# Causal attention whose exponentials are shifted by one maximum for four heads and 512 queries, with a checked general path

## The chip, the cores and the metric

The kernel runs on one core of one Trainium2 chip. The metric is the device time of one launch in microseconds. Five engines of the core work in parallel, each through its own instructions in program order: TensorE (PE in the profile, with its weight loads shown apart as PEld), VectorE (DVE), ScalarE (ACT), GpSimd (POOL) and SyncE (SP), which here issues almost all transfers. Three launches of the kernel before took 2398.28, 2401.68 and 2404.61 us.

## The reference, cut to what matters

The input has 4096 tokens of 256 features. An attention with 16 heads of 16 features and a feed-forward network follow each other, each between two layer norms and with a residual:

```python
qkv = x @ w_attn + b_attn
q, k, v = jnp.split(qkv, 3, axis=-1)              # then 16 heads of 16 features
logits = jnp.einsum('bhqd,bhkd->bhqk', q, k) * scale
logits = jnp.where(causal[None, None, :, :], logits, -jnp.inf)
weights = jax.nn.softmax(logits, axis=-1)
out = jnp.einsum('bhqk,bhkd->bhqd', weights, v)
return out.reshape(b, n, d) @ w_proj + b_proj
...
x = x + _layernorm(attention(_layernorm(x)))
x = x + _layernorm(feed_forward(_layernorm(x)))   # 256 -> 1024 -> 1024 -> 1024 -> 256
```

A softmax row doesn't change when one number is subtracted from all its logits before the exponentials. The number that is usually taken is the row's own maximum; any other number serves as long as the exponentials neither overflow nor all vanish. The logits of the reference's inputs, worked out from these inputs with the reference's own arithmetic, lie between about -0.75 and 0.75.

## The kernel before, in words

**Tiling.** The 4096 tokens are cut into 8 blocks `j` of 512 queries (`QB`), the 16 heads into 4 groups `g` of four heads. One *item* is a pair `(j, g)`; there are 32, done in the order of `j`, then `g`. An item runs over its keys in *key steps* `kt` of 128 keys: `4 (j + 1)` of them, since the attention is causal, and 576 in all. The last four key steps of an item lie on the diagonal and have 512, 384, 256 and 128 queries left.

**What one key step computes.** `ScoreUnit` (L711 on) makes the logits of two heads at a time, keys on the partitions and queries along the row; a key step has two such units. Its `products` (L729) issues for each head a product of keys and queries (`s<-q,k`) and accumulates a second product onto it (`s<-mrow,ones`): `mrow` holds minus the row maximum of every query, split in two halves, and the product with a tile of ones subtracts it from the logits. ScalarE then takes the exponential from PSUM to the tile `e` (L744), GpSimd zeroes the upper triangle on the diagonal (L749), and two key steps later `Values.step` (L779) multiplies `e` with the values of the four heads and accumulates into the PSUM tile `av`. A column of ones among the values gives the sum of the exponentials, in row 16 of each head's 32 rows. After an item's last key step `av` is copied (L789) and stored (L791).

**Where the row maxima come from.** Before an item's exponentials can start, the maxima of its rows must be known. `MaxUnit` computes the same logits once more with queries on the partitions (L624, tile `pm`, a ring of three PSUM banks) and reduces them along the keys on VectorE (L658; on the diagonal L662, a custom instruction that adds a mask and takes the maximum). In part of the key steps (`hold`, L643) ScalarE first copies one of the four banks to SBUF, and VectorE reduces the copy (L647); that happens only where no other work was lent to ScalarE since (`lent`). At the end of a query tile four maxima per row are combined (L675); at the end of an item they are split into halves (L681 to L686), and `to_rows` turns them to rows by four small products (L694, tile `pmt`) and a copy on ScalarE (L703, `mrow`).

**The order.** It is written out by hand. While item `n` runs, the maxima of item `n+1` are issued, one pair of `MaxUnit`s (four reductions) per key step, and `LEAD` = 3 pairs of the item after it. Per key step the program has: the first `MaxUnit`, two `ScoreUnit`s, the second `MaxUnit`, and the values of two key steps earlier. `to_rows` comes when the counter `now`, which rises by 2 per key step, has advanced by 4 since the maxima ended. `Background` puts pieces of other work between key steps: layer norm, q, k and v of the block two ahead (`prep`), projection and second layer norm of the last block (`project`), and a rounding of the feed-forward weights on GpSimd that sets a flag (`halve_weights`, `count_low`); some of these pieces run a `MaxUnit` beside them. SP's queue carries, in program order, the key and query loads (L495), the stores of q and k (L488), the stores of `av` (L791) and the transfers of `project`, whose sums go to DRAM and come back broadcast over partitions (L252, L257, L262).

**The end.** `feed_forward` is built twice, behind a branch on the flag: with weights that fit the fast fp32r format (`halves`), or without. The first is the one that runs here.

## Time and profile before

The profiled execution took 2401.19 us; its span is 2399.5 us, so 1.7 us lie around it, and it stands 0.5 us under the median of the three launches (2401.68 us). The table gives busy times in four parts of the span. The cuts are the starts of three copies of `av` (L789): that of the last item of block 1, of the last item but one, and of the last. Each copy starts some two key steps after its item's last one, so the count of key steps is meant to within two.

| part | us | PE busy | DVE busy | ACT busy | key steps |
|---|---|---|---|---|---|
| blocks 0 and 1, with the set-up | 269.68 | 220.33 | 158.94 | 123.72 | 48 |
| blocks 2 to 7, all items but the last | 1400.62 | 1378.63 | 1258.95 | 1170.82 | 496 |
| last item (no maxima left to compute) | 65.94 | 65.73 | 0.00 | 59.49 | 32 |
| feed-forward and end | 663.26 | 653.37 | 350.23 | 160.30 | - |
| profiled span | 2399.50 | | | | 576 |

Busy time is the union of an engine's instructions. Two instructions that follow each other without a wait overlap a little (the next starts before the results of the last are written), so the time from start to start is shorter than the duration that a row gives. Matmul ends are modelled.

### The profile page before, as it was taken

To read this page: it belongs to the slowest core of one execution; us is meant where nothing else is said; L and a number is where in the kernel's file an instruction comes from. 1 tells how busy PE (TensorE), PEld (TensorE's weight loads), DVE (VectorE), ACT (ScalarE), POOL (GpSimd) and SP (SyncE) were. 2 spreads that over 40 slices of the span, in tenths; PEclk is the share of its full clock that TensorE was granted. 3 is DMA by queue.
4 is the path that set the end of the run, shared out by engine and by line. 5 is a ranking of instruction groups with operands and counts; after the bars stand their busy time and mean duration, and the time that the engine had idled before them with its cause. 6 is when DMAs were issued, how large, how long until landed. Compare 5 with 4: busy or idle time off the path is not lost.

```text
span 2399.5 us, 40893 instructions
## 1 busy us (share of the span) xinstructions
PE 2318.1 (97%) x15237; PEld 1408.6 (59%) x15237; DVE 1768.1 (74%) x4102; ACT 1514.3 (63%) x2087; POOL 565.9 (24%) x898
## 2 busy tenths in 40 slices
PE   4889999999999999999999999999999999999998
PEld 2545554455554555545555555544488888888887
DVE  1667887998999899988999998986056546544653
ACT  1447787887797888888899888976822222222221
POOL 2324334432334223243223321010002100000000
PEclk8879999999999999999999999999999999999999
DMA  4443534433332432244323232111021000000000
GB/s 144 159 151 123 176 101 159 138 115 106 112 97 96 145 123 75 97 159 120 111 77 96 81 115 62 54 54 62 7 97 46 27 1 18 18 18 1 18 9 11
DMA packets 134831, 202.78 MB, mean 85 GB/s; under 512 B 14912, under 2 KB 59584, under 8 KB 134624
## 3 DMA queue, kind: packets, MB, share of 16 engines
q1 hardware_dynamic: 132672, 198.75, 25.4%
q8 instruction: 122, 2.00, 0.4%
q10 hardware_dynamic: 1776, 1.18, 0.2%
q14 instruction: 85, 0.70, 0.1%
q0 software_dynamic: 176, 0.15, 0.1%
HBM read 137.91 MB, written 62.13 MB: 83 GB/s over the span
## 4 chain that ended last, share of the span: by engine, by line
PE 87%; DVE 6%; ACT 2%; DMA 2%; POOL 1%; issue 1%; SPq 0%; ACTq 0%; POOLq 0%; DVEq 0%
PE av L779 21%; PE s L729 19%; PE z L1090 19%; PE pm L624 15%; PE pyf L1172 2%; PE za L1090 2%; PE zb L1090 2%; DVE mx L658 2%; DVE pm L662 2%; PE py L280 1%; PE pk L465 1%; PE pv L586 1%; PE pq L465 1%; PE pmt L694 1%; ACT e L744 1%
## 5 line engine op out<-in xcount | busy, mean ns | idle before, releaser
L744 ACT ACTIVATE e<-s 128x1024 f32<-128x1024 f32 (+3 forms) x1175 | 1039.7, 936 | 101.0 <-PE s L729 90.5
L658 DVE TENSOR_REDUCE mx<-pm 128x1 f32<-128x512 f32 x1496 | 963.1, 685 | 132.1 <-PE pm L624 90.8
L624 PEld LDWEIGHTS pm<-k,q 64*128 64x128 f32 x2304 | 301.2, 186 | 498.6 <-DVE mx L658 344.4
L624 PE MATMUL pm<-k,q 64*128 64x512 f32 (+3 forms) x2304 | 569.8, 439 | 22.8 <-DVE mx L658 11.7
L779 PE MATMUL av<-e,v 128*32 128x512 f32 (+3 forms) x4608 | 580.3, 575 | 0.6 <-POOL e L749 0.6
L729 PE MATMUL s<-q,k 64*128 64x512 f32 (+3 forms) x2304 | 465.2, 389 | 9.6 <-ACT e L744 2.0
L729 PE MATMUL s<-mrow,ones 64*128 64x512 f32 (+3 forms) x2304 | 452.6, 379 | 0.0
L1157 ACT ACTIVATE fb<-z,sh 128x512 f32<-128x512 f32 x128 | 88.3, 690 | 364.8 <-PE z L1090 339.5
L729 PEld LDWEIGHTS s<-q,k 64*128 64x128 f32 x2304 | 230.6, 187 | 79.8 <-issue 17.8
L662 DVE CUSTOM_DVE_ANT_0 pm<-pm,mask 128x128 f32<-128x128 f32 (+3 forms) x463 | 212.6, 499 | 73.1 <-PE pm L624 68.1
L749 POOL TENSOR_SCALAR_AFFINE_SELECT e<-e 128x256 f32<-128x256 f32 x256 | 103.0, 411 | 682.4 <-ACT e L744 680.7
L729 PEld LDWEIGHTS s<-mrow,ones 64*128 64x128 f32 x2304 | 234.3, 187 | 37.1 <-ACT mrow L703 0.5
L643 ACT COPY held<-pm 128x512 f32<-128x512 f32 (+1 forms) x345 | 200.2, 580 | 50.2 <-PE pm L624 17.7
L647 DVE TENSOR_SCALAR_CACHE_REDUCE held<-held 128x512 f32<-128x512 f32 x296 | 200.1, 676 | 0.1
L1090 PE MATMUL z<-hb_0h,h 128*128 128x512 f32 x512 | 199.3, 389 | 0.0
L1090 PE MATMUL z<-hb_0l,h 128*128 128x512 f32 x512 | 199.2, 389 | 0.0
L779 PEld LDWEIGHTS av<-e,v 128*32 128x32 f32 x4608 | 91.6, 108 | 145.5 <-issue 129.0
L202 POOL TENSOR_TENSOR rstd<-ve,neghalf 128x4 f32<-128x4 f32 (+1 forms) x22 | 20.8, 945 | 632.9 <-DVE ve L200 607.4
L1057 DVE CAST hb_1h<-fb 128x512 fp32r<-128x512 f32 x64 | 27.3, 427 | 156.0 <-ACT fb L1157 156.0
L1134 ACT ACTIVATE sl<-za,s 128x512 f32<-128x512 f32 x64 | 44.0, 690 | 120.0 <-PE za L1090 58.2
L1090 PEld LDWEIGHTS z<-hb_0l,h 128*128 128x128 f32 x512 | 96.1, 188 | 19.9
L1090 PEld LDWEIGHTS z<-hb_0h,h 128*128 128x128 f32 x512 | 96.1, 188 | 19.9
(251 smaller groups left out, 2553.6 us busy)
## 6 DMA issues: line engine op xcount, KB each, us to landing
k<-k SPq DMA_DIRECT2D x288, 256.0 KB
q<-q SPq DMA_DIRECT2D x64, 256.0 KB
x<-in_x_dram SPq DMA_DIRECT2D x16, 512.0 KB
k<-hik SPq DMA_DIRECT2D x32, 256.0 KB
k<-lok SPq DMA_DIRECT2D x32, 256.0 KB
q<-hiq SPq DMA_DIRECT2D x32, 256.0 KB
q<-loq SPq DMA_DIRECT2D x32, 256.0 KB
avd<-av_sb SPq DMA_DIRECT2D x32, 256.0 KB
```

The lines of the kernel that those rows point to most:

```text
L465: nc.tensor.matmul(ps, lhsT=wqk[d][:, i * D + c * P : i * D + (c + 1) * P], rhs=xTs[j][:, d, :], start=(d == 0), stop=(d == DC - 1),)
L624: nc.tensor.matmul(ps[:, 0:n], lhsT=qT[j, g][pr][r, t * P : (t + 1) * P], rhs=kT[G * j + g, c, pr][r, 0:n], start=True, stop=True,)
L643: nc.scalar.copy(held[:, 0:n], ps[:, 0:n])
L647: nc.vector.tensor_scalar(held[:, 0:n], held[:, 0:n], -3.0e38, None, ALU.max, ALU.max, accum_out=self.mx[:, h, c : c + 1],)
L658: nc.vector.tensor_reduce(self.mx[:, h, c : c + 1], ps[:, 0:n], AX.X, ALU.max)
L662: nc.vector.tensor_tensor_reduce(out=ps[:, 0:n], in0=ps[:, 0:n], in1=mask[:, QB - n : QB], scale=1.0, scalar=-3.0e38, op0=ALU.add, op1=ALU ...
L729: nc.tensor.matmul(self.ps[i][:, self.q0 :], lhsT=(self.k, ones[pr])[m][r, :], rhs=(qT[j, g][pr], mT[j, g])[m][r, self.q0 :], start=(m == ...
L744: nc.scalar.activation(e[:, at : at + n, q0:], ps[:, :, q0:], AF.Exp)
L749: nc.gpsimd.affine_select(out=at, in_=at, compare_op=ALU.is_ge, fill=0.0, base=0, pattern=[[0, 2], [1, P]], channel_multiplier=-1,)
L779: nc.tensor.matmul(self.av[h * HW : (h + 1) * HW, q0:], lhsT=vb[kt // NT][:, kt % NT, o : o + HW], rhs=es[h // 2][:, h % 2, q0:], start=(k ...
L1090: nc.tensor.matmul(ps, lhsT=w[c], rhs=single(part[:, c, :]), start=(c == 0 and i == 0), stop=(c == kc - 1 and i == parts - 1),)
L1157: nc.scalar.activation(h, z, AF.Gelu, scale=sc[:, oc : oc + 1])
```

## The change

The second product onto the logits goes, and with it the rows of maxima. An item gets one number for its four heads and 512 queries: the maximum over all the logits that `MaxUnit` computes (the mask on the diagonal goes too, so this includes keys after the query). It is applied as a per-partition bias of the exponential on ScalarE. To find it, VectorE reduces an item's maxima to one per partition (`col`), the 128 numbers go to DRAM and come back broadcast to all partitions (`all`), and VectorE reduces again with the sign turned (`shift`). The program now runs four pairs of maxima ahead instead of three, the last reduction comes 6 counts of `now` after the maxima instead of 4, and in the last two items one pair is issued in every key step until none is left.

Since one shift for many rows can let a row's exponentials vanish, the smallest entry of each row of `av` is kept (`least`), and early in the feed-forward it is tested against 2^-12 where the row is a sum (`tell_distant`). At the end the result is loaded into a register; if any sum was too small, the whole program is run once more by the attention with row maxima (the old code, now `attention(False)`) and the general feed-forward, both built into the same program behind that branch.

The diff without the lines that only moved to the right:

```diff
+        nc.vector.tensor_scalar(sums, sums, 1.0e-30, None, ALU.max)
         nc.vector.reciprocal(sums, sums)
...
+    def tell_distant():
+        nc.vector.tensor_reduce(close, least, AX.X, ALU.min)
+        nc.vector.tensor_scalar(close, close, LEAST, None, ALU.is_ge)
+        nc.vector.tensor_tensor(close, close, other, ALU.max)
+        yield True
+        nc.sync.dma_start(out=lows.rearrange("o p -> p o"), in_=close)
+        row = const.tile([1, P], F32, tag="row", name="row")
+        nc.sync.dma_start(out=row, in_=lows)
+        for _ in range(4):
+            yield True
+        total = stat.tile([1, 1], F32, tag="total", name="total")
+        nc.vector.tensor_reduce(total, row, AX.X, ALU.add)
+        nc.vector.tensor_scalar(distant, total, float(P), None, ALU.is_lt)
+        yield True
...
-    xT0 = []
+    def attention(shared):
+        xT0, W = [], {}
...
-        vb, qT, mT = [], {}, {}
+            ones, identr, mask = (None,) * 3 if shared else constants()
+            vb, qT, mT, shifts = [], {}, {}, {}
+            lead, WAIT = (4, 6) if shared else (LEAD, 4)
...
+                if shared:
+                    mx = top.tile([P, 4 * NT * NB], F32, tag="mx_all", name=f"mx_{j}_{g}")
+                    for t in range(NT):
+                        for c in range(j + 1):
+                            n = QB if c < j else (t + 1) * P
+                            yield [(j, g, t, c, pr, n, mx) for pr in (1, 0)]
+                    return
...
                     heads.append((h, held))
+                    if shared:
+                        return self.overall(heads, held if hold else None)
...
+                def overall(self, heads, held):
+                    j, g, t, c, pr = self.at
+                    mx, n = self.mx, self.n
+                    for h, ps in heads:
+                        at = 4 * (t * (j + 1) + c) + h
+                        if ps is held:
+                            nc.vector.tensor_scalar(
+                                ps[:, 0:n], ps[:, 0:n], -3.0e38, None, ALU.max, ALU.max,
+                                accum_out=mx[:, at : at + 1],
+                            )
+                        else:
+                            nc.vector.tensor_reduce(mx[:, at : at + 1], ps[:, 0:n], AX.X, ALU.max)
+                    if not (pr == 0 and self.diagonal and t == NT - 1):
+                        return False
+                    col = stat.tile([P, 1], F32, tag="col", name=f"col_{j}_{g}")
+                    nc.vector.tensor_reduce(col, mx[:, 0 : 4 * NT * (j + 1)], AX.X, ALU.max)
+                    nc.sync.dma_start(out=highest[j * G + g, :, None], in_=col)
+                    self.all = top.tile([P, P], F32, tag="all", name=f"all_{j}_{g}")
+                    nc.sync.dma_start(out=self.all, in_=highest[j * G + g].partition_broadcast(P))
+                    return True
+
             def to_rows(self):
+                    if shared:
+                        j, g = self.at[:2]
+                        shift = shifts[j, g] = stat.tile([P, 1], F32, tag="shift", name=f"shift_{j}_{g}")
+                        nc.vector.tensor_reduce(shift, self.all, AX.X, ALU.max, negate=True)
+                        return
...
-                for m in range(2):
+                    for m in range(1 if shared else 2):
...
-                            lhsT=(self.k, ones[pr])[m][r, :],
-                            rhs=(qT[j, g][pr], mT[j, g])[m][r, self.q0 :],
+                                lhsT=ones[pr][r, :] if m else self.k[r, :],
+                                rhs=(mT[j, g] if m else qT[j, g][pr])[r, self.q0 :],
                             start=(m == 0),
-                            stop=(m == 1),
+                                stop=(shared or m == 1),
...
-                    nc.scalar.activation(e[:, at : at + n, q0:], ps[:, :, q0:], AF.Exp)
+                        nc.scalar.activation(
+                            e[:, at : at + n, q0:],
+                            ps[:, :, q0:],
+                            AF.Exp,
+                            **({"bias": shifts[j, g]} if shared else {}),
+                        )
...
                     nc.sync.dma_start(out=weighed[j][g], in_=av_sb)
+                        if shared:
+                            at = j * G + g
+                            nc.vector.tensor_reduce(
+                                least[:, at : at + 1], av_sb, AX.X, ALU.min
+                            )
...
-                rows_due.append((now + 4, unit))
+                    rows_due.append((now + WAIT, unit))
...
-        while issued < first[1] + LEAD:
+            while issued < first[1] + lead:
...
-        rows_of(now + 4)
+            rows_of(now + WAIT)
...
                 due = begun + (goal - begun) * (kt + 1) // count[n] - issued
+                    if shared and goal == first[-1]:
+                        due = min(begun + kt + 1, goal) - issued
...
+                if j == 0 and tell:
+                    bg.add("distant", tell_distant(), 8)
...
+    ahead = attention(True)
     low = nc.values_load(flag, min_val=0, max_val=1)
     with tc.If(low < 1) as either:
-        feed_forward(True)
+        feed_forward(True, *ahead, True)
     with either.Else():
-        feed_forward(False)
+        feed_forward(False, *ahead, True)
+    far = nc.values_load(distant, min_val=0, max_val=1)
+    with tc.If(far > 0):
+        feed_forward(False, *attention(False))
```

## The prediction

> **What bounds the kernel now.** I read the page's busy times first, then busy times by stage, then one key step in the timeline.
>
> ```profile
> PE 2318.1 (97%) x15237; PEld 1408.6 (59%) x15237; DVE 1768.1 (74%) x4102; ACT 1514.3 (63%) x2087; POOL 565.9 (24%) x898
> ```
>
> PE looks like the only bound. But the change touches the attention alone, and there the shares are different (columns: us, then busy us and instructions of each engine; granted clock, DMA share, GB/s):
>
> ```profile
> 0.00:269.68 269.68, 220.33 (x1253) 118.88 (x1254) 158.94 (x512) 123.72 (x207) 91.55 (x160) 0.87 0.45 150
> 269.68:1670.30 1400.62, 1378.63 (x10342) 712.95 (x10340) 1258.95 (x2886) 1170.82 (x1576) 418.36 (x670) 1.00 0.32 104
> 1670.30:1736.24 65.94, 65.73 (x504) 25.98 (x500) 0.00 (x0) 59.49 (x85) 3.22 (x8) 0.99 0.02 9
> ```
>
> In the long middle part PE is 98% busy, DVE 90% and ACT 84%. So an edit that takes work from PE alone meets DVE soon. One key step of that part, in the timeline (start, us, engine, line):
>
> ```profile
> 1002.11 0.59 ACT L643 COPY held<-pm 128x512 f32<-128x512 f32 x1
> 1002.64 1.94 ACT L744 ACTIVATE e<-s 128x1024 f32<-128x1024 f32 x2
> 1002.75 0.68 DVE L647 TENSOR_SCALAR_CACHE_REDUCE held<-held 128x512 f32<-128x512 f32 x1
> 1003.17 1.06 PE L779 MATMUL av<-e,v 128*32 128x512 f32 x8
> 1003.35 2.08 DVE L658 TENSOR_REDUCE mx<-pm 128x1 f32<-128x512 f32 x3
> ...
> 1004.17 0.50 PE L624 MATMUL pm<-k,q 64*128 64x512 f32 x2
> 1004.50 0.39 PE L729 MATMUL s<-q,k 64*128 64x512 f32 x2
> 1004.70 0.59 ACT L643 COPY held<-pm 128x512 f32<-128x512 f32 x1
> 1004.74 0.39 PE L729 MATMUL s<-mrow,ones 64*128 64x512 f32 x2
> ```
>
> From one held copy to the next is 2.59 us. In it PE is busy all the time, DVE 2.49 us and ACT 2.47 us (the same busy times by stage, for 1002.11 to 1004.70). I call it a hold step; the middle part has 332 of them (count of L643 in it). All three engines are full there. The other 164 of its 496 key steps take 1400.62 - 332 x 2.59 = 541 us, 3.30 us each: those carry pieces of other work on PE, or are narrow.
>
> **The change, part by part.** All sums are against the profiled 2401.2 us, 0.5 below the median.
>
> *Taken from PE.* From 1004.50 to 1004.74 is 0.23 us for a pair of products, and a full key step has two pairs with `mrow`: 0.46 us. `pmt` (L694) takes 15.7 us of the middle part.
>
> *Added to ACT.* The exponential gets a bias that is read per partition. No exponential has one now. The nearest rows are the layer norm's passes, without and with such a bias, and a copy and an Identity with one:
>
> ```profile
> L643 ACT COPY held<-pm 128x512 f32<-128x512 f32 x322 | 189.1, 587 | 48.7 <-PE pm L624 17.7
> L180 ACT ACTIVATE junk<-y,mvy 128x256 f32<-128x256 f32 x28 | 14.2, 508 | 0.5
> L172 ACT ACTIVATE junk<-y 128x256 f32<-128x256 f32 x28 | 11.6, 416 | 0.7
> L474 ACT ACTIVATE fullk<-pk,bqk 128x512 f32<-128x512 f32 x16 | 11.0, 688 | 36.5 <-PE pk L465 36.5
> ```
>
> 508 - 416 = 92 ns and 688 - 587 = 101 ns. I take 93 ns per exponential; if an exponential's bias were free, the bound is 0. The middle part has 995 exponentials: +92.5 us on ACT, less 13.5 for the `mrow` copies (L703). ACT goes from 1171 to 1250 us.
>
> *DVE keeps its load.* The four reductions per key step stay. Gone are L675 (16.1 us in the middle part) and L681 to L686 (19.3 us in all 32 items, 14 in the 23 items here); added are 23 `least` reductions (as L647, 0.68: 16 us) and 46 small ones (as L675's, some 0.2: 9 us). On the diagonal a plain reduction of 512 (685 ns) stands for the masked one (711); narrower ones I take as 26 ns shorter too: 16 x 23 of them, -10 us. DVE stays near 1244 us. So the middle part, PE-bound at 1379 of 1401, becomes one with ACT 1250, DVE 1244 and PE about 1379 - 212 - 16 = 1151. (Each item has three narrow steps; the pairs there shrink with the queries, by some 0.70 us for the three together. 427 full steps x 0.46 plus 23 x 0.70 is 212.).
>
> *Hold steps (332).* ACT, without a wait, needs 0.53 (1002.11 to 1002.64) plus twice an exponential from start to start: 1.94 less the last one's 1.02 is 0.92, plus 0.093, so 2.56 us, against 2.59 now. Thus at best -0.03 x 332 = -10. If ACT's waits stay as they are, each step grows by 0.19: +62. I take -7, near the lower end, since what ACT waits for is PE, which now has 0.46 us to spare; DVE's 2.49 lies below.
>
> *The other 164 steps.* PE's saving there is 95 full steps x 0.46 + 23 x 0.70 = 60 us. Around an `mrow` copy two key steps took 1012.47 to 1018.38, 5.91 instead of 5.18; without it 0.73 x 23 = 17. Of these 77 us all come off if PE sets each of these steps, none if DVE does. DVE has 1259 - 332 x 2.49 = 432 of 541 us there; after -77 it would be 93% busy, more than work in such pieces reaches elsewhere in the part (90%). I take two thirds, -51; bounds -77 and 0.
>
> *The new wait.* `shift` waits on DVE, in program order, for two transfers through DRAM in sequence. Behind it stand all later reductions, and behind those the `pm` banks and PE; ACT's next item waits for the shift itself. SP holds its later loads meanwhile. No such tiny store exists; `project` sends sums the same way, in the chain of waits and in SP's timeline:
>
> ```profile
> 158.93 2.55 DMA sums<-avd
> 162.08 1.42 DMA invd<-sums
> ```
> ```profile
> 277.83 0.32 SPq L257 DMA_DIRECT2D invd<-sums x1
> 278.19 0.63 SPq L261 DMA_DIRECT2D oo<-avd x1
> 281.71 0.57 SPq L262 DMA_DIRECT2D To<-invd x1
> ```
>
> A store lands after 1.42 us, or as late as 281.71 - 277.83 = 3.88; a load takes 2.55. The round trip is 4.0 to 6.4 us. The count of 6 leaves two full key steps between `col` and `shift`, 5.2 us. The wait is 0 to 1.2 us, 23 times: 0 to 28. I take 0.4, 9 us, as most trips have the short store.
>
> The Trainium skill ("DMA: Bandwidth & Descriptors", Specifications) says that runs under 512 bytes are written by read-modify-write, which speaks against this store of 4-byte pieces. No row here shows its price. The same page (Anatomy of one DMA) gives some 2.0 us fixed per transfer for GpSimd's path; two would be an estimated 4.0 us and no wait.
>
> *The start (0 to 269.68).* Half of L729's 55.83 us there and 7.3 of `pmt` go from a PE that is 82% busy; I take 12 of these 35. The first shifts are needed at once: a round trip of 4.0 to 6.4 us, uncovered, where a product and a copy stood: +5. Together -7; bounds -30 and +8.
>
> *The last item.* ACT has 84 exponentials: 59.49 + 7.8 = 67.3 us, over the present 65.94: +2; bounds -2 and +8.
>
> *The end.* Each engine loads the flag and jumps over the general program; the present load took 0.5 us and PE's jump over the other feed-forward 3.8. Mostly beside the last store: +2; bounds 0 and +8. `tell_distant` runs in the feed-forward, where DVE is 53% busy: 0, or at most its 5 small operations.
>
> Sum: -7 - 51 + 9 - 7 + 2 + 2 = -52: **2349 us**.
>
> **The clock.** PE becomes sparser. The profile grants 0.57 at 132.59 to 156.13, where PE ran 100 products in 23.5 us (4.2 per us), but 1.00 at 213.08 to 248.77 with 214 in 35.7 (6.0 per us). A hold step will have 16 in 2.56 us, 6.2. I take no loss. The skill ("TensorE: Matmul & The Clock Gate", HAM oscillation) warns of PE gaps over about 3.4 us; the waits above are shorter.
>
> **The rivals.**
> - *ScalarE becomes the pole.* The held copy is ACT's own work, so in a hold step the waits for `pm` come after it and don't shrink: +62 instead of -7 gives 2418. For it: 2.56 against 2.59 leaves nothing for jitter. Against: PE's 0.46. It decides from 52/332 = 0.16 us more per hold step than the 2.57 I take, that is from 2.73 us.
> - *The round trip is late.* SP holds the store behind others that wait for GpSimd, or the small pieces are slow. At 10 us (the chain's 6.63 us for a broadcast load, `To`, plus 3.88) the wait is 4.8 x 23 = 110 instead of 9: 2450. It pays back the whole gain from (52 + 9)/23 = 2.7 us of wait, a trip of 7.9. Against: SP's other waits point to older instructions.
> - *PE's saving comes through.* The middle part at DVE's floor, 1259: -142, and the rest -3: 2256. Against: DVE idles now in spite of a full queue.
> - *The general path runs.* Then the time about doubles. The inputs' logits lie within 0.75, so a sum is at least e^-1.5 = 0.22, far above 2^-12. Under 0.005.
>
> **How the numbers follow.** Forecast (2290 to 2390) 0.56; PE's saving through 0.07; terms that cancel to within 0.3% (7 us, about what this measurement can tell) 0.08; ScalarE as pole 0.15; late round trip 0.14. Faster 0.56 + 0.07 = 0.63, same 0.08, slower 0.29. The range leaves out most of the saving-through case and the worse half of the late trips: 2290 to 2430.
>
> **What would show it.** L744's 1024-wide mean near 1115 ns; hold steps at 2.55 to 2.60 us; no `s<-mrow`; PE near 85% in the middle part, DVE and ACT both above 91%; idle time before `shift` on DVE of some 10 us. I am wrong if ACT's mean doesn't move, if hold steps pass 2.7, if DVE's idle before `shift` passes 60 us, or if the granted clock drops after 270 us.

## The result, and the profile after

The changed kernel takes 2749.46 us (median of four launches, 2737.81 to 2759.22) against 2401.93 us for the kernel before on the same chip: a ratio of 1.1446, 95% interval 1.1399 to 1.1493. It is slower by 14%; forecast were 2349 us, and 2290 to 2430 us as the range. The profiled execution has a span of 2756.8 us, 357 more than before; it lies 10 us above the median of the four launches.

Busy times by stage of the changed kernel, cut at the same three copies of `av` as before (columns: us; busy us and instructions of PE, PEld, DVE, ACT, POOL; granted clock, DMA share, GB/s):

```profile
0.00:365.60 365.60, 226.24 (x1024) 107.41 (x1024) 151.60 (x335) 126.27 (x198) 89.10 (x156) 0.74 0.35 113
365.60:2011.10 1645.50, 1443.44 (x8263) 567.78 (x8261) 1233.77 (x2488) 1226.01 (x1566) 413.36 (x669) 0.89 0.27 88
2011.10:2077.90 66.80, 65.73 (x376) 18.23 (x376) 0.69 (x1) 63.87 (x86) 3.22 (x8) 0.96 0.11 39
2077.90:2756.80 678.90, 656.58 (x3144) 552.12 (x3144) 351.92 (x712) 160.03 (x223) 53.01 (x61) 0.99 0.08 24
```

Against before, the start has 96 us more, the middle part 245, the last item 1 and the feed-forward with the end 16. In the middle DVE's and ACT's busy times are near what was forecast (1234 and 1226 us, for 1244 and 1250). But PE runs some 2000 products less and is busy 65 us *longer* (1443 for 1379), at a granted clock of 0.89 where it had 1.00, and it stands for 202 us of the part where it stood for 22. Nothing has become full; everything waits, and PE runs slowly besides.

What is waited for, from the view of waits of the same profile (engine, line, releaser: us in total, times, longest):

```profile
PEld pm L674 <- DVE mx L758: 704.0, 695, 9.2
DVE shift L773 <- DMA all<-highest: 243.3, 30, 20.0
PEld pm L674 <- ACT held L693: 86.8, 312, 1.0
DVE least L883 <- ACT av_sb L878: 92.3, 32, 66.1
PE pm L674 <- DMA k<-k: 72.5, 5, 29.7
```

The first row existed before (344.4 us in 480 waits); it has doubled, in good part because VectorE itself stands in the second (without the trip, in e3_on_chip below, the first row is 485.1 us). The kernel before has no wait like the last row's, of PE for keys. One stand of VectorE, in the timeline (start, us, engine, line, operation; in brackets the idle time before and its releaser):

```profile
1426.96 0.27 DVE L762 TENSOR_REDUCE col<-mx 128x1 f32<-128x112 f32 x1
...
1427.26 0.32 SPq L763 DMA_DIRECT2D highest<-col  x1
...
1431.75 0.50 PE L674 MATMUL pm<-k,q 64*128 64x512 f32 x2
...
1432.17 1.13 PE L292 MATMUL py<-wp,oo 128*128 128x256 f32 x4
...
1433.23 0.49 PE L674 MATMUL pm<-k,q 64*128 64x512 f32 x1
1434.79 0.32 SPq L765 DMA_DIRECT2D all<-highest  x1
1439.57 0.28 DVE L773 TENSOR_REDUCE shift<-all 128x1 f32<-128x128 f32 x1 [7.50 <-DMA all<-highest]
1439.77 2.47 DVE L758 TENSOR_REDUCE mx<-pm 128x1 f32<-128x512 f32 x4
...
1440.51 0.79 PE L674 MATMUL pm<-k,q 64*128 64x512 f32 x1 [6.78 <-DVE mx L758]
...
1441.23 2.07 PE L292 MATMUL py<-wp,oo 128*128 128x256 f32 x4
...
1443.23 0.79 PE L674 MATMUL pm<-k,q 64*128 64x512 f32 x2
```

SP issues the store of 128 numbers at 1427.26, and its next instruction, the load, goes out only when the store has landed: 1434.79, 7.53 us later. From the load's issue to `shift` it is 4.78 us. The whole trip is 12.3 us against 5.2 us of cover. VectorE stands for 7.50 us, and behind it PE for 6.78. After the stand the same products take longer: one pair of `pm` 0.79 instead of 0.50 us, four `py` products 2.07 instead of 1.13. The clock has fallen, and it stays at one half for the next 27 us, in which PE is busy again for 26.3 (the same columns as above):

```profile
1440.50:1467.40 26.90, 26.32 (x99) 11.73 (x99) 15.88 (x29) 12.01 (x20) 6.68 (x10) 0.50 0.46 156
1467.40:1480.00 12.60, 12.60 (x86) 4.78 (x82) 11.44 (x24) 11.91 (x14) 5.45 (x8) 1.00 0.21 69
```

Taken together, the trace's clock record has 582 us at half clock in this launch, in 43 stretches of 3.4 to 47.8 us; before, it has 88 us in 8.

SP's queue stands too, and the key loads behind it. The last row of the waits, at the second shift of block 0:

```profile
120.29 0.32 SPq L763 DMA_DIRECT2D highest<-col  x1
127.81 0.32 SPq L765 DMA_DIRECT2D all<-highest  x1
128.62 0.79 SPq L537 DMA_DIRECT2D q<-q  x2
129.46 1.32 SPq L537 DMA_DIRECT2D k<-k  x2
...
136.39 0.47 PE L674 MATMUL pm<-k,q 64*128 64x128 f32 x2 [17.01 <-DMA k<-k]
```

The loads of the next keys stand in the program behind the store, which has to wait for `col`, and behind the load of the maxima, which waits 7.52 us for the store; PE stands for 17.01 us. In the start PE stands 64.9 us in four such places.

The Trainium skill ("TensorE: Matmul & The Clock Gate", HAM oscillation), which the forecast set aside because its waits were to be short, warns of gaps over about 3.4 us; the trace agrees, with a gap of 6.78 us and products at 0.79 for 0.50 us behind it, and by the clock record 28 of the launch's 30 gaps over 5 us have the clock fall to one half, in the gap or within 3.5 us behind it.

### The profile page after: what moved, and what is told of

It reads as the page before. It is cut to its first block, busy times and chain, and to the rows that moved or that the text cites. A ratio compares the mean times of both kernels' runs of the same rounds, so it can differ in the third digit from the quotient of the medians.

```text
span 2756.8 us, 35602 instructions
## 1 busy us (share of the span) xinstructions
PE 2392.0 (87%) x12805; PEld 1245.6 (45%) x12805; DVE 1738.0 (63%) x3535; ACT 1576.2 (57%) x2069; POOL 558.7 (20%) x894
## 4 chain that ended last, share of the span: by engine, by line
PE 68%; DMA 17%; DVE 8%; ACT 4%; issue 2%; POOL 1%; SPq 0%; ACTq 0%; POOLq 0%; DVEq 0%
PE av L868 17%; PE z L1189 17%; PE pm L674 15%; DMA highest<-col 9%; PE s L813 8%; DMA all<-highest 5%; DVE mx L758 5%; PE pyf L1273 2%; PE za L1189 2%; PE zb L1189 2%; ACT e L828 2%; PE py L292 1%; PE pk L507 1%; PE pv L628 1%; DVE held L748 1%
## 5 line engine op out<-in xcount | busy, mean ns | idle before, releaser
L758 DVE TENSOR_REDUCE mx<-pm 128x1 f32<-128x512 f32 (+3 forms) x1946 | 1151.4, 633 | 317.0 <-PE pm L674 263.2
L828 ACT ACTIVATE e<-s,shift 128x1024 f32<-128x1024 f32 (+4 forms) x1176 | 1142.9, 1038 | 237.0 <-PE s L813 207.6
L674 PE MATMUL pm<-k,q 64*128 64x512 f32 (+3 forms) x2304 | 758.1, 491 | 280.7 <-DVE mx L758 204.7
L674 PEld LDWEIGHTS pm<-k,q 64*128 64x128 f32 x2304 | 354.8, 201 | 927.5 <-DVE mx L758 704.0
L868 PE MATMUL av<-e,v 128*32 128x512 f32 (+3 forms) x4608 | 639.9, 617 | 1.9 <-POOL e L838 1.0
L813 PEld LDWEIGHTS s<-q,k 64*128 64x128 f32 x2304 | 240.2, 203 | 181.5 <-ACT e L828 119.8
L748 DVE TENSOR_SCALAR_CACHE_REDUCE held<-held 128x512 f32<-128x512 f32 (+1 forms) x358 | 239.0, 668 | 0.5
L773 DVE TENSOR_REDUCE shift<-all 128x1 f32<-128x128 f32 x32 | 9.1, 285 | 243.3 <-DMA all<-highest 243.3
L929 POOL CAST wh<-wc 128x256 fp32r<-128x256 f32 x88 | 34.9, 396 | 295.1 <-DMA wc<-in_h_t_dram 203.9
L1156 DVE CAST hb_0h<-fb 128x512 fp32r<-128x512 f32 x64 | 27.5, 430 | 95.5 <-ACT fb L1258 95.5
```

Source lines behind the costliest of these rows:

```text
L674: nc.tensor.matmul(ps[:, 0:n], lhsT=qT[j, g][pr][r, t * P : (t + 1) * P], rhs=kT[G * j + g, c, pr][r, 0:n], start=True, stop=True,)
L748: nc.vector.tensor_scalar(ps[:, 0:n], ps[:, 0:n], -3.0e38, None, ALU.max, ALU.max, accum_out=mx[:, at : at + 1],)
L758: nc.vector.tensor_reduce(mx[:, at : at + 1], ps[:, 0:n], AX.X, ALU.max)
L813: nc.tensor.matmul(self.ps[i][:, self.q0 :], lhsT=ones[pr][r, :] if m else self.k[r, :], rhs=(mT[j, g] if m else qT[j, g][pr])[r, self.q0 ...
L828: nc.scalar.activation(e[:, at : at + n, q0:], ps[:, :, q0:], AF.Exp, **({"bias": shifts[j, g]} if shared else {}),)
L868: nc.tensor.matmul(self.av[h * HW : (h + 1) * HW, q0:], lhsT=vb[kt // NT][:, kt % NT, o : o + HW], rhs=es[h // 2][:, h % 2, q0:], start=(k ...
```

## The experiments

All times are medians; each ratio is to the kernel before on the same chip (between 2399 and 2402 us), with its 95% interval. Stages (us of each profiled span) are cut like those above. They are of one launch each, which lies up to 11 us off its run's median (10 and 7 above it for the changed kernel and e3_on_chip, 11 and 7 below it for e6_dummy_product and e11_lead_of_before), so a difference of a few us between the stages of two runs tells nothing by itself. The diffs show the lines that matter: `...` stands for others between them, and lines of less weight, such as those that make a tile or set a flag, aren't shown.

| run | time | ratio | start | middle | last | rest |
|---|---|---|---|---|---|---|
| before | 2401.93 | 1 | 269.7 | 1400.6 | 65.9 | 663.2 |
| changed kernel | 2749.46 | 1.1446 [1.1399, 1.1493] | 365.6 | 1645.5 | 66.8 | 678.9 |
| e1_later_shift | 2577.25 | 1.0731 [1.0711, 1.0751] | 350.7 | 1480.4 | 66.1 | 681.3 |
| e2_more_lead | 2584.56 | 1.0764 [1.0742, 1.0787] | 381.7 | 1457.0 | 66.9 | 678.4 |
| e3_on_chip | 2453.01 | 1.0217 [1.0200, 1.0234] | 296.0 | 1414.8 | 66.0 | 681.0 |
| e4_bias_alone | 2411.22 | 1.0049 [1.0033, 1.0065] | 270.0 | 1408.3 | 66.1 | 663.1 |
| e5_no_product | 2385.73 | 0.9940 [0.9917, 0.9962] | 269.4 | 1391.1 | 59.7 | 663.0 |
| e6_dummy_product | 2458.18 | 1.0243 [1.0226, 1.0260] | 285.8 | 1413.4 | 65.5 | 679.9 |
| e7_one_run | 2535.90 | 1.0569 [1.0544, 1.0594] | 308.2 | 1481.9 | 65.2 | 680.4 |
| e8_chip_no_bias | 2439.32 | 1.0157 [1.0137, 1.0178] | 288.2 | 1411.2 | 58.2 | 679.2 |
| e9_tell_on_chip | 2447.29 | 1.0200 [1.0183, 1.0217] | 291.1 | 1413.8 | 66.0 | 671.6 |
| e10_defer_least | 2400.06 | 1.0001 [0.9991, 1.0011] | 282.7 | 1378.8 | 66.0 | 671.3 |
| e11_lead_of_before | 2387.86 | 0.9955 [0.9940, 0.9970] | 265.3 | 1377.3 | 65.3 | 670.4 |
| e12_first_keys | 2282.59 | 0.9514 [0.9498, 0.9530] | 300.0 | 1243.5 | 65.6 | 671.7 |

**Is it the trip?** The theory was that the trip through DRAM, longer than its cover, costs nearly everything. Two runs give it more cover, one takes it away.

e1_later_shift, on the changed kernel:

```diff
-            lead, WAIT = (4, 6) if shared else (LEAD, 4)
+            lead, WAIT = (4, 10) if shared else (LEAD, 4)
...
-                rows_of(now + 2)
+                rows_of(now + (14 if shared else 2))
```

> The changed kernel with the shift's reduction 10 counts after the maxima instead of 6 (four key steps of cover, 10.4 us, instead of two); nothing else moves, but that an item's own shift is always taken before its first key step. Theory: the round trip of 12 to 13 us against 5.2 us of cover is the loss, so the wait before the shift falls from some 8 us to 2 to 3 us per item and the time from 2749 to 2430 to 2530 us. Rival (ScalarE's longer exponentials are the loss): the wait falls as well but the time stays above 2650 us.

e2_more_lead, on the changed kernel:

```diff
-                        rows_due.append((now + WAIT, unit))
+                        rows_due.append((now + (14 if shared and unit.at[:2] >= (1, 0) else WAIT), unit))
...
-                goal = min(first[min(n + 2, len(items))] + lead, first[-1])
+                goal = min(first[min(n + 2, len(items))] + (6 if shared and n >= 2 else lead), first[-1])
...
-                rows_of(now + 2)
+                rows_of(now + (14 if shared else 2))
```

> The changed kernel with six pairs of lead instead of four (from block 0's third item on) and the reduction 14 counts after the maxima, six key steps or 15.6 us of cover. Theory: the wait before the shift is gone but for the first items, TensorE's granted clock stays at 1.00 after block 1, and the time is 2350 to 2430 us. Rival (ScalarE): above 2600 us. A second rival, that the two transfers hurt by holding up SP's queue and not VectorE: the wait before the shift goes to 0, but the time stays above 2550 us.

e3_on_chip, on the changed kernel: no transfer; a product with the identity spreads `col` over all partitions.

```diff
-                    nc.sync.dma_start(out=highest[j * G + g, :, None], in_=col)
-                    self.all = top.tile([P, P], F32, tag="all", name=f"all_{j}_{g}")
-                    nc.sync.dma_start(out=self.all, in_=highest[j * G + g].partition_broadcast(P))
+                    self.col = col
...
-                        nc.vector.tensor_reduce(shift, self.all, AX.X, ALU.max, negate=True)
+                        ps = two_banks(f"all_{j}_{g}")[:, 0, 0:P]
+                        nc.tensor.matmul(
+                            ps, lhsT=self.col.to_broadcast([P, P]), rhs=ident, start=True, stop=True
+                        )
+                        nc.vector.tensor_reduce(shift, ps, AX.X, ALU.max, negate=True)
```

> The changed kernel without the round trip: one product with the identity spreads the 128 maxima over all partitions into PSUM, and VectorE reduces from there. Lead and counts as in the change. Theory: 2330 to 2400 us, the forecast's own sum without its wait; no transfer of maxima, clock 1.00 after block 1. Rival (ScalarE): 2418 us or more, with hold steps above 2.7 us.

More cover brought 172 and 165 us, less than the theory expected of either: VectorE's wait before `shift` fell from 243.3 to 101.2 and 90.7 us, but the blocks 0 and 1, with four and eight key steps in an item, have little to put into a longer cover, and their stage stays at 351 and 382 us. e2_more_lead's second rival (SP's queue hurts, not VectorE: above 2550 us) is in part right. In that run's middle part VectorE waits for a shift in one place only, 12.9 us, and yet this part is 42 us longer than e3_on_chip's; in 27.0 of them PE waits for keys. In the whole launch PE waits for keys 130.8 us in e2_more_lead, 74.6 in e1_later_shift, 72.5 in the changed kernel and 14.8 in e3_on_chip: a longer cover did nothing for the loads that stand in SP's queue. Without the trip the time falls by 296 us. So the trip is shown to be the cause of most of the loss, but not of all: 2453 us lies above what was expected, and above the kernel before. The rival's time is met (2418 or more), its reason isn't: hold steps are 2.59 us and not above 2.7. In the middle part of e3_on_chip, busy times by stage are

```profile
295.98:1710.82 1414.84, 1366.39 (x8310) 537.52 (x8307) 1235.89 (x2488) 1225.49 (x1566) 414.11 (x669) 0.98 0.31 102
```

Against the changed kernel 230.7 us have gone: PE stands 48.5 us instead of 202.1 (154 us), and for the same products it is busy 1366 instead of 1443 (77 us). By this account two thirds of the trip's price here are the stand, one third the slower products that follow it.

**Which part of the trip?** e7_one_run, on the changed kernel, turns `col` on TensorE to one row first, so that the store writes one run of 512 bytes instead of 128 pieces of 4:

```diff
-                    nc.sync.dma_start(out=highest[j * G + g, :, None], in_=col)
+                    turned = two_banks(f"col_{j}_{g}")[:, 0, 0:P]
+                    nc.tensor.transpose(turned[0:1, :], col, ident)
+                    line = stat.tile([1, P], F32, tag="line", name=f"line_{j}_{g}")
+                    nc.vector.tensor_copy(line, turned[0:1, :])
+                    nc.sync.dma_start(out=highest[j * G + g : j * G + g + 1, :], in_=line)
```

> The changed kernel, round trip kept, but the 128 maxima are first turned into one row by TensorE and stored as one run of 512 bytes. Theory (the store is slow because it consists of 128 pieces of 4 bytes): from its issue to the issue of the load 1.4 to 2.5 us instead of 7.4 to 8.6; the wait before the shift falls from 8 to 2 to 3 us per item and the time to 2500 to 2560 us. Rival (the trip is slow because SP's queue is full): the store still takes 7 us, time above 2700.

PE, VectorE and SP in its timeline:

```profile
1343.53 0.27 PE L764 MATMUL col<-ident,col 128*1 128x128 f32 x1 [1.83 <-DVE col L762]
1343.83 0.28 DVE L766 COPY line<-col 1x128 f32<-1x128 f32 x1 [0.45 <-PE col L764]
1344.14 0.24 SPq L767 DMA_DIRECT2D highest<-line  x1
1345.22 0.32 SPq L769 DMA_DIRECT2D all<-highest  x1
...
1351.43 0.28 DVE L777 TENSOR_REDUCE shift<-all 128x1 f32<-128x128 f32 x1
```

The store now lands 1.08 us after its issue instead of 7.53, and VectorE waits 10.9 us before `shift` in all instead of 243.3. So the small pieces are the greater part of the trip, and the 512 bytes in themselves are not. Nor is it the number of pieces: `project`'s store in the kernel before (`invd<-sums`, 32 KB from 128 partitions, by its code 128 pieces of 256 bytes) lets SP issue the load behind it 1.44 to 1.52 us after its own issue in five of its eight places (2.7, 3.9 and 30.6 us in the others, the last with a wait for PE in it). What is slow is 128 pieces of 4 bytes. By the trace's record of packets the 128 of 4 bytes are moved 1.0 us after the issue, and what the other 6.5 us until the landing are spent on isn't shown. The time, 2536 us, is still 83 above e3_on_chip; the view of waits has 55 us in which PE waits for `col` before it turns it (53 us of its weight load fall in the same places), and 83 us weren't taken apart further.

**What do the two halves of the change bring alone?** e4_bias_alone is the kernel before with a bias of zeros; e5_no_product is the kernel before without the second product; e8_chip_no_bias is e3_on_chip without the bias.

```diff
-                    nc.scalar.activation(e[:, at : at + n, q0:], ps[:, :, q0:], AF.Exp)
+                    nc.scalar.activation(e[:, at : at + n, q0:], ps[:, :, q0:], AF.Exp, bias=zero)
```

> The kernel before, whose exponentials take a tile of zeros as their per-partition bias: the added ScalarE work alone. Theory: the mean of a 1024-wide exponential goes from 1022 to about 1115 ns, ScalarE is busy some 109 us longer, and of this 10 to 40 us show, since it has 0.12 us to spare per hold step and more elsewhere: 2410 to 2440 us. Rival (ScalarE is the pole): 0.19 us for each of 528 key steps show, 2490 to 2510 us.

```diff
-                for m in range(2):
+                for m in range(1):
```

> The kernel before without the second product on the logits; the row maxima are still computed and turned into rows, but not subtracted. TensorE's saving alone. My forecast's theory (the waits of ScalarE and VectorE shrink when TensorE has time): hold steps 2.51 to 2.57 us, time 2330 to 2370. Rival (the ring of three pm banks closes a loop: held copy, second pm product, values, next pm product, held copy, 2.59 us with or without the second product): hold steps stay at 2.59 us, the saving shows only in the other steps, and where TensorE is left idle the granted clock falls: 2380 to 2420 us.

```diff
-                            **({"bias": shifts[j, g]} if shared else {}),
```

> The on-chip shift (e3) whose exponentials don't take it as their bias (the shift is computed and not applied): e3 less the added ScalarE work. Theory (ScalarE is not the pole): 10 to 25 us under e3's 2453, hold steps still 2.59 us. Rival (ScalarE's waits set the hold step): hold steps fall below 2.52 us and the time below 2400.

The bias costs 93 ns an exponential and 12 us in all (e8_chip_no_bias gets 14 back):

```profile
L746 ACT ACTIVATE e<-s,zero 128x1024 f32<-128x1024 f32 x939 | 997.2, 1115 | 38.4 <-PE s L731 34.8 <-POOL e L751 0.5 <-POOL fit L837 0.4
```

That row is of e4_bias_alone (mean 1115 ns; the kernel before has 1022). The second product, of which the forecast took 212 us off PE, is worth 16 us (2385.73 for 2401.62 on its chip), 6 of them in the last item. The steps between held copies stay as they were: their median in the middle part (steps under 3 us) is 2.590 us before, 2.593 in e3_on_chip, and 2.591 in the changed kernel, e4_bias_alone, e5_no_product and e8_chip_no_bias. e5_no_product in the timeline:

```profile
1003.42 0.50 PE L624 MATMUL pm<-k,q 64*128 64x512 f32 x2
1003.95 0.59 ACT L643 COPY held<-pm 128x512 f32<-128x512 f32 x1 [0.16 <-PE pm L624]
...
1004.59 0.18 PEld L624 LDWEIGHTS pm<-k,q 64*128 64x128 f32 x1 [0.41 <-ACT held L643]
1004.60 0.67 DVE L647 TENSOR_SCALAR_CACHE_REDUCE held<-held 128x512 f32<-128x512 f32 x1
1005.02 1.06 PE L779 MATMUL av<-e,v 128*32 128x512 f32 x8
...
1005.20 1.28 DVE L658 TENSOR_REDUCE mx<-pm 128x1 f32<-128x512 f32 x2
...
1006.01 0.50 PE L624 MATMUL pm<-k,q 64*128 64x512 f32 x2
```

These lines close to a ring. PE makes `pm`; ScalarE copies it 0.53 us after its start; the copy ends, and 0.05 us later PE may load the weights of the product into the bank that came free (a wait of 0.41 us; this kind of wait is 131.3 us in 337 places here and stood in no place before); then come that product, the values (1.06 us after the copy's start, before and after the change, in e5_no_product and in e8_chip_no_bias), and 1.00 us behind these the next `pm`. 0.53 + 1.06 + 1.00 = 2.59 us. VectorE goes round with it: copy, held reduction 0.65 later, plain reduction 0.60 later and 0.69 long, next `pm` 0.12 after its end, copy 0.53 after that, 2.59 again. At the ends of long stands PE goes on 0.05 us after VectorE's reduction; here it is 0.12, so PE's side seems to close the ring, but no run took that apart. Neither side holds the second product or an exponential, and taking either away left the step as it was (e5_no_product, e8_chip_no_bias). Before, PE filled those 0.46 us with the product; now it waits for the copy in them. How much the ring costs is another matter: VectorE's four reductions are busy 2.49 of the 2.59 us, before and in e5_no_product, so without a ring they alone would still hold the step near 2.49 (an estimate from these rows). No run took VectorE's work alone away, and the ring and VectorE's load aren't told apart.

**Does the clock cost anything by itself?** e6_dummy_product is e3_on_chip with the second product put back, with weights of zero:

```diff
-                    for m in range(1 if shared else 2):
+                    for m in range(2):
...
-                                lhsT=ones[pr][r, :] if m else self.k[r, :],
+                                lhsT=(idle if shared else ones[pr])[r, :] if m else self.k[r, :],
```

> The on-chip shift (e3) with a second product kept in place of the one removed, with weights of zero: TensorE's load as before, nothing else. Theory (a sparser TensorE loses its clock): the granted clock after block 1 returns to 1.00 and the time falls below e3's 2453 us although there is more work: 2415 to 2440. Rival (the clock only follows the waits and costs nothing): 2453 us or more, up to 2470.

The mean clock rises (median of the launches 0.973 for 0.960; in the profiled middle part 1.00 for 0.98), and the time doesn't fall (2458 for 2453 us, launches of 2447 to 2461 for 2453 to 2460). So a sparser PE does lose some clock here, and filling it up gains nothing. The run doesn't tell whether the lost clock was free or the added products cost what it gave back.

**What is left without the trip?** Three terms, each on top of the run before it. e9_tell_on_chip takes `tell_distant`'s transfers away, e10_defer_least moves a reduction a few key steps down VectorE's program, e11_lead_of_before takes the lead and row counts of the kernel before.

```diff
-        nc.sync.dma_start(out=lows.rearrange("o p -> p o"), in_=close)
-        row = const.tile([1, P], F32, tag="row", name="row")
-        nc.sync.dma_start(out=row, in_=lows)
-        for _ in range(4):
-            yield True
+        ps = room.bank("pclose")
+        nc.tensor.transpose(ps[0:1, 0:P], close, ident)
+        yield True
...
-        nc.vector.tensor_reduce(total, row, AX.X, ALU.add)
+        nc.vector.tensor_reduce(total, ps[0:1, 0:P], AX.X, ALU.add)
```

> e3_on_chip with tell_distant's two transfers through DRAM (a store of 4-byte pieces and its load, 13.7 us in the chain of e3's feed-forward) replaced by a transpose on TensorE into PSUM. Theory: those transfers hold VectorE in program order and cost the feed-forward some 16 us; its stage falls from 681 to about 664 us, the median to about 2437 (2430 to 2443). Rival: the feed-forward is longer for another reason (the last item's later end, the clock) and stays at 675 or more; median 2447 to 2455.

```diff
-                            at = j * G + g
-                            nc.vector.tensor_reduce(
-                                least[:, at : at + 1], av_sb, AX.X, ALU.min
-                            )
+                            ended.append((now + 3, j * G + g, av_sb))
...
+            def keep_least(limit):
+                while ended and ended[0][0] <= limit:
+                    _, at, av_sb = ended.popleft()
+                    nc.vector.tensor_reduce(least[:, at : at + 1], av_sb, AX.X, ALU.min)
...
+                    keep_least(now)
```

> e9_tell_on_chip with each item's `least` reduction issued on VectorE a few key steps after the item's last value copy, so that VectorE no longer waits for that copy at once. Theory: the wait (96 us in 32 places in e3_on_chip) held up the maxima of the item ahead; most of it was on the path, and 15 to 35 us go: 2400 to 2422. Rival: the maxima are ahead by enough, the wait costs nothing, and the time is that of e9_tell_on_chip, within 7 us.

```diff
-            lead, WAIT = (4, 6) if shared else (LEAD, 4)
+            lead, WAIT = LEAD, 4
```

> e10_defer_least with the lead and the row counts of the kernel before (3 and 4 in place of 4 and 6). Theory: with the row mean on the chip there is no trip to cover, and the larger lead costs only at the start, where four items' maxima stand ahead of the first exponentials: the start falls from about 296 to some 275 us and the rest stays, 2380 to 2405. Rival: the start is set by something else, the time stays within 7 us of e10_defer_least or the shorter lead lets the maxima be late in the middle part, 2405 to 2440.

`tell_distant`'s store is the small-piece store again. In the changed kernel's chain of waits, in the feed-forward:

```profile
2090.88 12.19 DMA lows<-close
2103.09 2.59 DMA row<-lows
```

It holds VectorE for 11.8 us. Without it the rest falls from 681.0 to 671.6 us, about half of what was expected (664); in the seven runs with this store it is 678 to 681 us, in the four without it (e9 to e12) 670 to 672; the median moves by 6 us, lies 4 above the theory's bound and within the rival's 2447 to 2455. Some 8 us remain over before. In e10_defer_least, where they are the same, 2.1 of them lie ahead of the first product of `z`, where PE now waits 1.8 us to turn VectorE's test into a row, and 4 behind SP's branch on the rounding flag: 8.1 us from there to the end instead of 4.2, with the load of the new flag and the second branch between. The other 2 weren't placed.

`least` was the larger one. In e9_tell_on_chip's timeline, at an item's end:

```profile
1293.10 0.58 ACT L877 COPY av_sb<-av 128x512 f32<-128x512 f32 x1
...
1293.72 0.69 DVE L882 TENSOR_REDUCE least<-av_sb 128x1 f32<-128x512 f32 x1 [1.88 <-ACT av_sb L877]
1294.32 2.48 DVE L755 TENSOR_REDUCE mx<-pm 128x1 f32<-128x512 f32 x4
1295.06 0.49 PE L671 MATMUL pm<-k,q 64*128 64x512 f32 x1 [1.06 <-DVE mx L755]
```

VectorE stands 1.88 us for the copy, the maxima behind it are late, and PE waits for these. 31 such waits of 0.4 to 3.0 us make only 31 us (the 32nd, of the last item, delays nothing); deferring the reduction took 47 us off the time, more than the 15 to 35 that were expected, as the slower products behind such waits went too (in the middle part PE stands 28.0 instead of 48.5 us and is busy 1350.75 instead of 1365.36). The lead gave another 12 us, in the profiles nearly all of it in the start (265.3 for 282.7 us; these two launches lie 20 us apart, the medians 12). So e11_lead_of_before, which is the change without its transfers and its two waits, beats the kernel before by 0.45%. Its first two stages:

```profile
0.00:265.30 265.30, 207.87 (x1038) 100.06 (x1038) 149.07 (x331) 124.88 (x197) 88.83 (x156) 0.87 0.46 153
265.30:1642.56 1377.26, 1345.91 (x8313) 529.58 (x8311) 1236.38 (x2489) 1221.79 (x1561) 413.67 (x670) 1.00 0.32 104
```

**Is the ring the pole?** e12_first_keys takes the ring's load away, and with it most of VectorE's: beside the lines shown, no other work carries a `MaxUnit` any more, and the pairs are spread over the key steps by their new number.

```diff
-                        for c in range(j + 1):
-                            n = QB if c < j else (t + 1) * P
-                            yield [(j, g, t, c, pr, n, mx) for pr in (1, 0)]
+                        n = QB if j else (t + 1) * P
+                        yield [(j, g, t, 0, pr, n, mx) for pr in (1, 0)]
...
-                        hold = not (lent or xT0) and unit.n > QB // 2 and kt <= NT * j
+                        hold = not shared and not (lent or xT0) and unit.n > QB // 2 and kt <= NT * j
```

> e10_defer_least with the maxima taken of the first 512 keys only (16 maxima per partition and item instead of up to 16 per block of keys), no copies of scores by ScalarE (`held`), and the sums checked from above too (at most 1e30) as well as from below; the general attention stays behind the same branch. Theory: the ring of three banks with its copies, products and reductions set the key step of 2.59 us; without it ScalarE's two exponentials of 1.03 us do, about 2.1 us, and the middle part falls from 1415 to between 1050 and 1150 us: 1980 to 2090 in all. Rival: TensorE's clock falls once its work is sparser, or the pieces of other work set the key step: 2150 to 2300.

2282.59 us, 4.9% under the kernel before (ratio 0.9514 [0.9498, 0.9530]) and the fastest of all runs, though 193 us above the theory's upper end: the rival's range holds it. Late in the middle part the theory's step is there, with ScalarE's exponentials back to back, eight in 8.50 us:

```profile
1499.43 8.50 ACT L830 ACTIVATE e<-s,shift 128x1024 f32<-128x1024 f32 x8
```

Key steps of the last blocks take 2.16 to 2.34 us. But those of blocks 2 to 5, which carry the other work, take 2.4 to 3.9, and both of the rival's reasons are seen, without being told apart:

```profile
0.00:299.96 299.96, 208.78 (x940) 98.77 (x940) 111.55 (x229) 119.67 (x184) 88.95 (x156) 0.76 0.40 135
299.96:1543.47 1243.51, 1089.31 (x6615) 361.10 (x6615) 266.60 (x473) 1051.73 (x1218) 412.92 (x670) 0.95 0.36 115
```

ScalarE is busy 85% of the middle part, and PE's clock is 0.95 there and 0.76 in the start, which takes 17 us more than in e10_defer_least. The last blocks show that the maxima's work set the step, but not whether by the ring or by its size: in the middle part VectorE's load fell from 1233 to 267 us, PE's from 1351 to 1089 and ScalarE's from 1225 to 1052.

## Why the prediction was wrong, point by point

- **The new wait (+9 us, bounds 0 to 28): the step that failed.** "I take 0.4, 9 us, as most trips have the short store" took the stores of `project` for the nearest row. That row's store has as many pieces, 128, but of 256 bytes. A store of 128 pieces of 4 bytes takes 7.5 us, not 1.42 to 3.88, and the load to its use 4.8, not 2.55: 12.3 us instead of 4.0 to 6.4. The place, the engine and what stands behind it were right; the size wasn't, and in the middle part the term is 231 us (changed kernel less e3_on_chip) instead of 9. The rival of the late round trip was the right one, with its mechanism of small pieces, and its turning point of 7.9 us was passed; it too was too small, since it took a trip of 10 us and priced the stand alone, and left out the slower products after each stand, the start, and SP: "SP holds its later loads meanwhile" stands in the forecast without a term, and PE waited 72.5 us for keys, where without the trip it waited 14.8.
- **A rule was set beside the sum and outvoted.** The Trainium skill ("DMA: Bandwidth & Descriptors", Specifications) says that below 512 bytes a transfer does read-modify-write. It pointed the right way: 7.5 us for 128 pieces of 4 bytes, 1.1 us for the same 512 bytes in one run. But 128 pieces of 256 bytes, also under 512 each, landed within 1.5 us in most places of the kernel before, and that read-modify-write is the reason no run shows. The same page (Anatomy of one DMA) gives the fixed cost from which the forecast estimated 4.0 us for two transfers; this has nothing for the size of a piece, and the trace has 12.3 us.
- **Hold steps (-7): the reason failed.** "What ACT waits for is PE, which now has 0.46 us to spare." ACT's copy waits for a product that waits for the copy before it; steps stayed at 2.590 us before and 2.591 after. The count was off besides: of the 332 held copies only 282 are followed by the next one within 3 us, so that the other steps are 214 and not 164 (some 671 us, 3.1 each). The lines of the ring stood in the forecast's own timeline: copy 1002.11, values 1003.17, `pm` 1004.17, copy 1004.70. PE, DVE and ACT near 2.5 of 2.59 us were read as three full engines; one chain passes through all three, and of the three only DVE's load stays a possible floor of the step, at 2.49, since taking PE's or ACT's work away moved nothing.
- **The other steps (-51, bounds -77 to 0): right in sign, too large.** Cleared of trip, wait and lead, the middle part of e11_lead_of_before is 23 us shorter than before, hold steps and all. The second product alone gave 10 there (e5_no_product).
- **`least` was priced as work (16 us of DVE) and not as a wait.** It stands in VectorE's program right behind a copy that isn't made yet: some 35 us in the middle and 8 at the start (e9_tell_on_chip to e10_defer_least). The forecast asked the question of what is queued behind a wait for `shift`, and not for this one.
- **The start (-7, with +5 for the trip).** The trip costs 70 us here (365.6 to 296.0), as 48 short key steps hold eight trips and little cover; 50 of the 70 are PE waiting for keys behind SP's queue (64.9 us for 14.8). The longer lead, not priced at all, costs 12 us by the medians, 17 by the two profiled starts. Without both and with `least` deferred the start is 265.3 us, 4 under before, which one launch each can't tell from no change.
- **The end and `tell_distant` (+2 and 0).** The store between its operations cost 9 us. Another 8 stay, of which 6 were placed, 4 of them at the end of the program; the operations alone weren't taken out.
- **The bias (+93 ns): right.** 1022 became 1123 ns in the changed kernel and 1115 in e4_bias_alone. The last item: +2 forecast, +1 measured.
- **The clock ("I take no loss"): wrong, by way of the wait.** With some 6 products per us the middle part had 0.98 in e3_on_chip and 1.00 in e11_lead_of_before, as the forecast took from its rows (e12_first_keys, with 5.3, had 0.95); the changed kernel, with its stands, had 0.89. The forecast named the rule on gaps and found its gaps short.
- The tests named ahead fell the right way: idle time before `shift` was to stay by 10 us and refute the forecast above 60, and was 243.3 us; the clock was not to drop after 270 us, and did (0.89 in the middle part).

## What to carry to other kernels

Price a store by the size of its separate pieces, and not by its bytes or their number alone: take for the nearest row one with pieces as small. When no row shows such a one, let the sum bear the worst case before an engine with ring buffers behind it is made to wait for it. For each instruction that is put into a full engine's program, also the small ones, ask what it waits for where it stands; here moving it down a few steps was free. Ask also which loads stand in the same queue behind a transfer that waits. Three engines that are each nearly busy may be tied in one loop through a buffer: follow the chain from one copy to the next, and see whether the work to be removed lies in it, before its time is taken off the total.

## What the runs showed of the hardware

- A store of 128 four-byte pieces from 128 partitions to one row in DRAM took 7.5 us from its issue to its landing (12.2 us for the one in the feed-forward); the same bytes as one run took 1.1 us, and 128 pieces of 256 bytes at most 1.5 us in five places of eight (`invd<-sums` of the kernel before).
- After a stand of 6.78 us TensorE's products took 0.79 for 0.50 us and 2.07 for 1.13, and the granted clock stayed at 0.50 for 27 us more although TensorE was busy 98% of them. The mean granted clock of the whole profiled launch fell to 0.895 from 0.982.
- A per-partition bias adds 93 ns to an exponential of 1024 columns (1022 to 1115), and a product of one column, spread by a broadcast operand, with the identity hands 128 numbers to all partitions without a transfer: VectorE's wait before `shift` was 14 us in all, for 243.
